# Two attention blocks on one core: group means through DRAM, the output bias on VectorE, a split first norm, earlier q blocks, and the first two scores together

## The chip, the core and the metric

The kernel runs on one core of one Trainium2 chip. All times are device microseconds (us) of that core. The engines are named as in the profile: PE is TensorE (matrix products; PEld is its weight loads), DVE is VectorE, ACT is ScalarE, POOL is GpSimd and SP is SyncE, which here only issues transfers (its queue is SPq). All data are fp32.

## What is computed

Two self-attention blocks follow each other on x of shape 8 x 512 x 32 x 32 (8 images, 512 channels, 1024 positions). Both have the same form, cut here to what matters:

```
def block(x, gamma, beta, wqkv, bqkv, wp, bp):        # x: (8, 512, 1024)
    xg   = x.reshape(8, 8, -1)                        # 8 groups of 64 channels
    mean = xg.mean(-1, keepdims=True)
    var  = xg.var(-1, keepdims=True)
    xn   = ((xg - mean) * rsqrt(var + 1e-5)).reshape(x.shape) * gamma + beta
    q, k, v = split(wqkv @ xn + bqkv)                 # 8 heads of 64 channels each
    attn = softmax(q.T @ k / 8)                       # over the keys
    o    = attn @ v
    return x + wp @ o + bp
```

The whole is `block(block(x, weights of layer 0), weights of layer 1)`.

## The kernel before

A **job** is one image in one layer. There are 16, ordered so that two images alternate: image 0 and 1 in layer 0, then both in layer 1, then images 2 and 3, and so on. The order of PE, ACT and DVE instructions is written out by hand: each of these engines executes them in the order in which the Python code emits them. A small planner helps. `later(delay, fn)` (L104) registers work for a planned clock time, and `advance(us)` (L107) moves that clock by the planned length of the PE work just emitted and emits what has come due. SP's and POOL's order isn't written out; a scheduler arranges it by dependencies and priority.

A job goes through four stages.

- **V phase** (`v_phase`, L371). The value projection is computed with seven products of half-size blocks instead of eight (Strassen's scheme in Winograd's form). `combine` (L277) makes the sums of blocks of the normalised input on DVE, `factor` (L147) the sums of weight blocks. Seven products by two groups of tokens give 14 steps, each planned at 1.72 us. While such sums of a weight are first made, the raw blocks are loaded, four DVE operations turn them into seven factors, and `store_factors` (L158) keeps the result in DRAM, from where `fetch` (L165) loads single factors into a ring of 8 buffers.
- **Projection phase** of the job before (`proj_phase`, L405): the output projection in the same scheme. It adds `out_bias`, a vector per layer that holds bp + wp @ bv.
- **Deep phase** (`deep_phases`, L442): the K and Q projections with the scheme applied twice, so 7 + 7 chains of seven products of 128x128 by 128x256. Two chains are interleaved. `prepare` (L184) makes a chain's inner factors (four small DVE operations) when they are used for the first time. In each chain (`chain`, L328) product 7 is added up in bank z, a put reads z, and product 4 is then added up in the same bank. The puts of products 7 and 3 are on DVE, the others on ACT.
- **Attention** (`Attention`, L582): 8 groups (4 head pairs by 2 halves of the queries) of 8 key chunks, 64 steps. `scores(i)` (L592) emits the scores product `sc`, the exponential `e` on ACT and, from the second chunk of a group on, the DVE addition into `acc` (L611, L613) for the softmax sums; `values(i)` (L615) emits the product `po` with v. `finish` (L632) turns a group's sums into reciprocals by way of two small transfers (`lr`, `rd`) and a broadcast (`rb`), and normalises q's columns in place. Work of the next job is inserted into the 64 steps as `chores`, keyed by step.

The group norm of job n+1 runs as chores in the attention of job n (`norm_steps`, L208). `stat` (L221) makes mean and variance of each channel on DVE, for one chunk of 128 channels at a time. `group_mean` (L226) multiplies by the block matrix `blk`, whose 64x64 blocks hold 1/64: a product `pm` for the mean and, with the deviations, a product `pvar` for the variance. Each uses a `sc` buffer of PSUM. POOL takes the power -1/2, DVE scales (L253) and ACT adds beta (L260).

`make_out_bias` (L742) computes wp @ bv with 16 products of 128x128 by 128x1, into `pb`, again a `sc` buffer. It runs as a chore of jobs 0 and 2.

The start (from L777) issues the loads of image 0, the V and K blocks and image 1; does the whole norm of job 0 alone; emits the first four of the 14 V steps, then the sums and factors, then the rest. The raw q blocks are loaded later (`second_blocks`, L816) into the buffer of raw k, whose tag `"k"` the first K result uses as well.

The end of a deep phase and the start of the attention are interleaved, with `both[-3:]` the products 7, 3 and 4 of the last chain:

```
896         att = Attention(att_n)
897         att.scores(0)
898         both[-3]()
899         att.scores(1)
900         both[-2]()
901         both[-1]()
```

Of the kernel before, what the change touches and what calls it, by code (L numbers as in the profile page):

```python
# [9 lines left out]
F32 = mybir.dt.float32  # L10
# [28 lines left out]
NW = 7  # L39
# [5 lines left out]
RING = 8  # L45

# [9 lines left out]
def make_constants(nc, const, env, vecs):  # L56
    env.vec_sb = const.tile([P, 2 * NVEC], F32, name="vec_sb")
    nc.sync.dma_start(env.vec_sb, vecs)
# [11 lines left out]
def fast_path(  # L70
    ctx: ExitStack, tc: tile.TileContext, env: Env, x: bass.AP, wqkv: list, wp: list,
    out: bass.AP,
# [92 lines left out]
    def fetch():  # L165
# [9 lines left out]
        src = factors[which, layer][:, FACTOR[o]]  # L175
        if which in (V, O):
            nc.sync.dma_start(wide(w), src)
        elif (which, layer, o) in deep:
            nc.sync.dma_start(w, deep[which, layer, o])
        else:  # L180
            nc.sync.dma_start(wide(w), src)
            raw.add(key)
# [19 lines left out]

    def load_x(b):
        xs[b] = xpool.tile([P, NC, S], F32, tag="x", name=f"x_{b}")
# [3 lines left out]
    def norm_steps(n, alone=False):  # L208


        b, layer = jobs[n]
        xt = xs[b]
        stats = small.tile([P, NC, 2, 6], F32, tag="stats", name=f"stats_{n}")
        mv = small.tile([P, NC, 2], F32, tag="mv", name=f"mv_{n}")
        dev = small.tile([P, NC], F32, tag="dev", name=f"dev_{n}")
        mean = small.tile([P, NC], F32, tag="mean", name=f"mean_{n}")
        var = small.tile([P, NC], F32, tag="var", name=f"var_{n}")
        mul = small.tile([P, NC], F32, tag="mul", name=f"mul_{n}")
        g0 = layer * NVEC + GAMMA

        def stat(cc):  # L221
            for sh in range(2):
                nc.vector.bn_stats(stats[:, cc, sh, :], xt[:, cc, sh * HALF : (sh + 1) * HALF])
            nc.vector.bn_aggr(mv[:, cc, :], stats[:, cc, :, :].rearrange("p s k -> p (s k)"))

        def group_mean(src, name):  # L226
            if alone:
                pm = bank(0, "z", name)
                nc.tensor.matmul(pm[:, :NC], env.blk, src, start=True, stop=True)
                return [(slice(0, P), pm[:, :NC])]  # L230
            pm = two_banks("sc", name)
            for h in range(2):
                r = slice(h * HD, (h + 1) * HD)
                nc.tensor.matmul(pm[r, h, :NC], env.blk[r, r], src[r], start=True, stop=True)
            return [(slice(h * HD, (h + 1) * HD), pm[h * HD : (h + 1) * HD, h, :NC]) for h in range(2)]

        def first():
# [909 lines left out]
```

## Time and profile before

| | |
|---|---|
| median of 3 runs | 3291.85 us (3286.91 to 3293.28) |
| the profiled execution | 3291.33 us, span 3289.6 us, mean granted PE clock 0.996 |
| PE busy | 3265.8 us, 99% of the span |
| DVE busy | 2588.4 us, 79% |
| ACT busy | 1729.2 us, 53% |
| POOL busy | 17.5 us, 1% |
| transfers | 262.80 MB, mean 80 GB/s |
| scores products `sc` (L602) | 1070.1 us busy, 8192 instructions |
| values products `po` (L627) | 1059.1 us busy, 8192 instructions |
| group-mean products `pm` and `pvar` in attention (L234) | 120 instructions of 0.17 to 0.20 us |
| output-bias products `pb` (L749) | 64 instructions of 0.25 us |
| first V product | at 16.54 us |
| first scores product | at 92.46 us |
| V phase to V phase, jobs 4 and 5 | 828.30 to 1030.78 us |

A product of fp32 operands shows as two PE instructions. The ends of matmuls in the profile are modelled, so distances between starts say more than durations. In lines of a timeline the columns are start in us, duration in us, engine, line, operation, output<-input, shape and count; what stands in brackets is the idle time of the engine before it and what released it. In lines of the table of waits the columns are the waiting engine, line and instruction, what it waited for, us in total, number of waits and the longest.

### The profile page before, as it was taken

To read this page: it belongs to the slowest core of one execution; us is meant where nothing else is said; L and a number is where in the kernel's file an instruction comes from. 1 tells how busy PE (TensorE), PEld (TensorE's weight loads), DVE (VectorE), ACT (ScalarE), POOL (GpSimd) and SP (SyncE) were. 2 spreads that over 40 slices of the span, in tenths; PEclk is the share of its full clock that TensorE was granted. 3 is DMA by queue.
4 is the path that set the end of the run, shared out by engine and by line. 5 is a ranking of instruction groups with operands and counts; after the bars stand their busy time and mean duration, and the time that the engine had idled before them with its cause. 6 is when DMAs were issued, how large, how long until landed. Compare 5 with 4: busy or idle time off the path is not lost.

```text
span 3289.6 us, 56485 instructions
## 1 busy us (share of the span) xinstructions
PE 3265.8 (99%) x22420; PEld 1748.7 (53%) x22420; DVE 2588.4 (79%) x3630; ACT 1729.2 (53%) x2557; POOL 17.5 (1%) x30
## 2 busy tenths in 40 slices
PE   8999999999999999999999999999999999999999
PEld 6456374563745637356373564735546365563643
DVE  7886978869688696877959779596895968869676
ACT  3555635556364563646636366463654636546363
POOL 0000000000000000000000000000000000000000
PEclk9999999999999999999999999999999999999999
DMA  7223142140411203023050221303214031130401
GB/s 279 83 80 114 66 144 74 52 145 22 162 31 59 86 19 117 28 76 118 22 171 22 76 66 34 113 17 110 85 35 161 19 93 49 41 105 22 127 28 45
DMA packets 142352, 262.80 MB, mean 80 GB/s; under 512 B 44544, under 2 KB 52736, under 8 KB 141056
## 3 DMA queue, kind: packets, MB, share of 16 engines
q1 hardware_dynamic: 142080, 259.12, 24.7%
q8 instruction: 178, 2.92, 0.4%
q14 instruction: 94, 0.77, 0.1%
HBM read 212.10 MB, written 44.83 MB: 78 GB/s over the span
## 4 chain that ended last, share of the span: by engine, by line
PE 97%; ACT 1%; DMA 1%; DVE 1%; issue 0%; SPq 0%; POOL 0%; DVEq 0%
PE sc L602 27%; PE po L627 26%; PE vd L486 8%; PE zd L486 7%; PE z L384 6%; PE z L419 6%; PE ud L486 3%; PE yd L486 3%; PE u L384 2%; PE y L384 2%; PE v L384 2%; PE u L419 2%; PE y L419 2%; PE v L419 2%; ACT e L607 1%; PE pp L571 1%
## 5 line engine op out<-in xcount | busy, mean ns | idle before, releaser
L607 ACT ACTIVATE e<-sc 128x1024 f32<-128x1024 f32 x1024 | 1047.4, 1023 | 626.5 <-PE sc L602 545.3
L602 PE MATMUL sc<-q,k 64*64 64x512 f32 x8192 | 1070.1, 593 | 6.6 <-ACT e L607 6.6
L627 PE MATMUL po<-e,v 64*64 64x512 f32 x8192 | 1059.1, 590 | 0.0
L613 DVE TENSOR_TENSOR acc<-acc,e 128x1024 f32<-128x1024 f32 x768 | 936.5, 1219 | 60.6 <-ACT e L607 11.0
L627 PEld LDWEIGHTS po<-e,v 64*64 64x64 f32 x8192 | 313.6, 133 | 568.1 <-issue 557.9
L602 PEld LDWEIGHTS sc<-q,k 64*64 64x64 f32 x8192 | 305.7, 133 | 548.5 <-issue 524.8
L486 PE MATMUL vd<-deep,w 128*128 128x256 f32 x960 | 269.7, 382 | 0.0
L486 PE MATMUL zd<-deep,w 128*128 128x256 f32 x832 | 233.0, 380 | 3.9 <-DVE p L502 3.9
L611 DVE TENSOR_TENSOR acc<-e,e 128x1024 f32<-128x1024 f32 x128 | 156.1, 1219 | 66.5 <-ACT e L607 65.5
L486 PEld LDWEIGHTS vd<-deep,w 128*128 128x128 f32 x960 | 181.7, 191 | 37.2 <-ACT p L498 13.0
L486 PEld LDWEIGHTS zd<-deep,w 128*128 128x128 f32 x832 | 158.1, 190 | 33.3 <-issue 6.9
L639 DVE TRANSPOSE_TENSOR_REDUCE r<-acc 128x32 f32<-128x1024 f32 x128 | 158.5, 1238 | 0.5
L335 ACT COPY yd<-vd 128x256 f32<-128x256 f32 x128 | 45.7, 357 | 187.0 <-PE vd L486 180.1
L426 DVE TENSOR_TENSOR s5o<-v,x 128x512 f32<-128x512 f32 x60 | 38.5, 684 | 101.3 <-PE v L419 101.3
L419 PE MATMUL z<-to,w 128*128 128x512 f32 x240 | 110.3, 592 | 0.0
L384 PE MATMUL z<-w,xn 128*128 128x256 f32 x480 | 110.1, 382 | 0.0
L384 PE MATMUL z<-w,t 128*128 128x256 f32 x480 | 108.5, 379 | 0.0
L419 PE MATMUL z<-q,w 128*128 128x512 f32 x240 | 107.9, 592 | 0.0
L669 DVE TENSOR_TENSOR q<-q,rb 128x512 f32<-128x512 f32 x128 | 86.6, 676 | 26.5 <-DMA rb<-rd 26.5
L384 PEld LDWEIGHTS z<-w,xn 128*128 128x128 f32 x480 | 90.0, 190 | 23.8 <-issue 12.2
L339 ACT COPY u<-z 128x512 f32<-128x512 f32 x62 | 35.3, 570 | 121.5 <-PE z L419 84.8
L384 PEld LDWEIGHTS z<-w,t 128*128 128x128 f32 x480 | 91.2, 190 | 12.4
(169 smaller groups left out, 3434.4 us busy)
## 6 DMA issues: line engine op xcount, KB each, us to landing
w<-deep SPq DMA_DIRECT2D x196, 448.0 KB, 3.3
w<-keep SPq DMA_DIRECT2D x238, 256.0 KB, 2.7
rb<-rd SPq DMA_DIRECT2D x256, 128.0 KB, 2.9
x<-x_dram SPq DMA_DIRECT2D x32, 512.0 KB, 6.2
out_dram<-x SPq DMA_DIRECT2D x64, 256.0 KB, 3.5
deep<-w SPq DMA_DIRECT2D x28, 448.0 KB, 2.9
keep<-raw SPq DMA_DIRECT2D x5, 1792.0 KB, 6.0
lr<-r SPq DMA_DIRECT2D x512, 4.0 KB, 1.7
```

Source lines behind the costliest of these rows:

```text
L335: nc.scalar.copy(y, z)
L384: nc.tensor.matmul(ps[:, ti * CH : (ti + 1) * CH], r[:, cc, t0 : t0 + P], w[:, cc, :], start=(start and ti == 0 and cc == 0), stop=(cc == ...
L419: nc.tensor.matmul(ps, w[:, cc, i * P : (i + 1) * P], r[:, cc, :], start=(start and cc == 0), stop=(cc == 1), skip_group_check=True,)
L426: nc.vector.tensor_add(s5[:, oh, :], ps, at(oh, 1))
L486: nc.tensor.matmul(ps, lhs[:, FACTOR[i], :], moving[i], start=start, stop=True, skip_group_check=True,)
L602: nc.tensor.matmul(sc[h * HD : (h + 1) * HD, j, :], k[r, hp, k0 : k0 + HD], q[r, hp, sh * HALF : (sh + 1) * HALF], start=True, stop=True,)
L607: nc.scalar.activation(e, sc, AF.Exp, scale=SCALE)
L611: nc.vector.tensor_add(acc[g], es[i - 1], e)
L613: nc.vector.tensor_add(acc[g], acc[g], e)
L627: nc.tensor.matmul(po[g][j * HD : (j + 1) * HD, h, :], v[r, kc, d0 : d0 + HD], e[r, j, :], start=(kc == 0), stop=(kc == NT - 1),)
L639: nc.vector.tensor_reduce(r, a.rearrange("p j (b e) -> p (j b) e", e=RP), AX.X, ALU.add, apply_transpose=True,)
L669: nc.vector.tensor_mul(q[:, hp, cols], q[:, hp, cols], rb)
```

## The change

1. **Group means.** For jobs 1 to 15, `norm_steps` no longer uses PE. A new chore at step 17 (`gather`) stores the channels' means and variances to DRAM and loads them back with a group's 64 channels in one row, on 8 partitions. At step 24 (`groups`) DVE makes mean and variance of each group, POOL takes the power, a transfer stores the 8 pairs to DRAM and two broadcasts bring them back to all partitions. Scaling starts at step 36 as before.
2. **Output bias.** `make_out_bias` loads the rows of wp and a broadcast bv into the buffers `acc` and `px`, and DVE multiplies and reduces, four times per layer. It is called after the attention of jobs 0 and 2 and comes due 19 us into the next V phase.
3. **Start.** Image 0 is loaded in half chunks, the first two chunks ahead of one V block and the vectors; then the other chunks and V blocks, K's and the raw q blocks, these into the buffer of image 1, whose own load moves to 30 us later on the planned clock. The norm of job 0 is made in two halves of 2 chunks each, with PE products as before (of 2 columns), and idle products of `blk` between them; the first V step stands before the second half's norm. The V steps run in the order 1, 5, 2, 6, 7, 3, 4. One sum of V's weights moves to POOL. The first K and Q fetches of factors 1, 2 and 4 read the input weights instead of the stored factors. K and Q go into one plan; the sums for chain products on combined inputs come 12 us into it instead of 7.5.
4. **First scores.** `att.scores(0)` and `att.scores(1)` are called one after the other, before the last three products of the deep phase.

```
@@ norm @@
+        def gather(self):
+            self.dm = dram.tile([NC, P, 2], F32, tag="dm", name=f"dm_{self.n}")
+            nc.sync.dma_start(self.dm.rearrange("c p k -> p c k"), self.mv)
+            self.gm = small.tile([GROUPS, HD, 2], F32, tag="gm", name=f"gm_{self.n}", bufs=1)
+            nc.sync.dma_start(self.gm, self.dm.rearrange("c (h p) k -> (c h) p k", h=2))
+
+        def groups(self):
...
+            nc.vector.bn_stats(gs, gm[:, :, 0])
+            nc.vector.bn_aggr(ga, gs)
+            nc.vector.tensor_reduce(gv, gm[:, :, 1], AX.X, ALU.add)
+            nc.vector.tensor_scalar(gv, gv, 1.0 / HD, EPS, ALU.mult, ALU.add)
+            nc.vector.tensor_add(gv, gv, ga[:, 1:2])
+            nc.gpsimd.tensor_tensor(ga[:, 1:2], gv, env.neg_half[:GROUPS, 0:1], ALU.pow)
+            dg = dram.tile([GROUPS, 2], F32, tag="dg", name=f"dg_{n}")
+            nc.sync.dma_start(dg, ga)
             for h in range(2):
...
+                src = dg.rearrange("(c h) k -> h c k", h=2)[h : h + 1]
+                nc.sync.dma_start(
+                    self.mr[h * HD : (h + 1) * HD], src.to_broadcast([HD, NC, 2])
+                )
@@ output bias @@
+        for i in range(2):
+            nc.sync.dma_start(
+                rows[i], wrows[layer][i * CH : (i + 1) * CH].rearrange("(oc p) c -> p oc c", p=P)
+            )
+        nc.sync.dma_start(bvb, bv[layer : layer + 1, :].to_broadcast([P, C]))
+
+        def part(oc):
+            r = rows[oc // 2][:, oc % 2, :]
+            nc.vector.tensor_mul(r, r, bvb)
+            nc.vector.tensor_reduce(out_bias[:, layer, oc : oc + 1], r, AX.X, ALU.add)
...
-                nc.tensor.matmul(
-                    pb[:, 0, oc : oc + 1], w[:, at, cc % 2, o0 : o0 + P],
-                    env.vec(layer, BV, cc), start=(cc == 0), stop=(cc == NC - 1),
-                )
...
+            if n in (0, 2):
+                make_out_bias(jobs[n][1], 19.0)
@@ start @@
+    load_chunk(0)
+    load_chunk(1)
+    env.load_vecs()
+    load_block(v0, V, 0, 0)
+    load_chunk(2)
+    load_chunk(3)
+    for i, j in ((1, 0), (1, 1), (0, 1)):
+        load_block(v0, V, i, j)
     load_blocks(k0, 0, K)
-    load_x(1)
+    load_blocks(q0, 0, Q)
...
+    norm.stat(0)
+    norm.stat(1)
+    mean, var = norm.means_by_products(0, lambda: idle_products(0, "y", "again_a"))
+    mean()
+    var()
+    for i in range(3):
+        idle_products(i % 2, "y", f"again_b{i}")
+    norm.stat(2)
+    norm.factors(slice(0, 2))
+    normed((0, 1), left)
+    normed((0, 1), right_)
+    nc.gpsimd.tensor_add(v0[:, S1], v0[:, S3], v0[:, A22])
+    norm.stat(3)
+    first[0]()
+    mean, var = norm.means_by_products(1, lambda: None)
...
+    deep_sums(0, 0.2, 12.0)
+    later(5.0, first_plan)
     for part in range(4):
...
+        later(16.0 + 0.9 * part, lambda part=part: factor(q0, part))
+    later(20.0, lambda: store_factors(q0, 0, Q))
+    later(21.0, lambda: store_factors(v0, 0, V))
+    later(30.0, lambda: load_x(1))
@@ first scores @@
         att.scores(0)
-        both[-3]()
         att.scores(1)
-        both[-2]()
-        both[-1]()
+        for thunk in both[-3:]:
+            thunk()
```

## The prediction

> **What bounds the kernel now.** I read the busy times and the chain of waits first, then the table of waits of TensorE (PE), then the timeline around each place that the change touches.
>
> ```profile
> PE 3265.8 (99%) x22420; PEld 1748.7 (53%) x22420; DVE 2588.4 (79%) x3630; ACT 1729.2 (53%) x2557; POOL 17.5 (1%) x30
> PE 97%; ACT 1%; DMA 1%; DVE 1%; issue 0%; SPq 0%; POOL 0%; DVEq 0%
> PE sc L602 <- ACT e L607: 6.6, 30, 0.2
> PE zd L486 <- DVE p L502: 3.9, 3, 3.4
> PE z L384 <- ACT xn L259: 3.6, 1, 3.6
> PE vd L486 <- DMA w<-keep: 1.5, 1, 1.5
> ```
>
> PE is the bound. VectorE (DVE) at 79% and ScalarE (ACT) at 53% lie beside it. Three of the four waits belong to the first 75 us; the fourth is 30 short stops at the group-mean products. So an edit is worth the PE time that it takes away, or the PE stop that it makes.
>
> A whole job (an image and a layer) takes 202.48 us from one V phase to the next (828.30 to 1030.78 in the chain in order of time). Around a group-mean product the timeline of PE reads (start, duration):
>
> ```profile
> 344.47 1.04 PE L627 MATMUL po<-e,v 64*64 64x512 f32 x8
> 345.33 0.24 PE L234 MATMUL pm<-mv,blk 64*64 64x4 f32 x4
> 345.80 1.09 PE L602 MATMUL sc<-q,k 64*64 64x512 f32 x8 [0.22 <-ACT e L607]
> 346.70 1.04 PE L627 MATMUL po<-e,v 64*64 64x512 f32 x8
> 347.74 1.09 PE L602 MATMUL sc<-q,k 64*64 64x512 f32 x8
> ```
>
> Groups normally start 0.858 us apart. The output-bias product of job 0, in the same view:
>
> ```profile
> 117.69 1.04 PE L627 MATMUL po<-e,v 64*64 64x512 f32 x8
> 118.66 4.68 PE L749 MATMUL pb<-vec_sb,raw 128*128 128x1 f32 x32
> 123.27 1.98 PE L602 MATMUL sc<-q,k 64*64 64x512 f32 x8
> 126.74 1.69 PE L602 MATMUL sc<-q,k 64*64 64x512 f32 x8
> ```
>
> And two windows at the start (stretch; PE, PEld, DVE, ACT and POOL busy; PEclk; DMA):
>
> ```profile
> 59.79:63.20 3.41, 1.20 (x6) 1.07 (x7) 3.38 (x9) 0.82 (x3) 0.00 (x0) 1.00 0.87 284
> 63.20:66.61 3.41, 3.41 (x10) 2.70 (x9) 2.94 (x8) 1.07 (x4) 0.00 (x0) 0.50 0.94 358
> ```
>
> After a stretch of 3.41 us in which PE worked 1.20 us (35%), the next 3.41 us ran at half clock.
>
> **What the Trainium skill says.** "TensorE: Matmul & The Clock Gate", section Part 1 (What's actually happening): a free-running window of 3413 ns sets the clock, which halves after an idle window and returns after a busy one. The trace agrees on the length and the factor, but 35% busy was already idle enough. "DMA: Bandwidth & Descriptors", Anatomy of one DMA: a fixed cost of about 2.0 us, mostly the write's receipt; here the 4 KB stores rd<-rt land in 1.3 us and lr<-r in 1.7. "Perfetto Trace Analysis", Tensor Engine Instruction: DVE and ACT are strict FIFO. This decides the last edit below.
>
> **Group means.** Each pm puts the later groups off: sc at 347.74 should, with 0.858 spacing, have been at 347.05, and the po after it (348.65) at 347.90, so 0.75 us. Each pvar the same way: po 361.18 against 360.67, 0.51. The 15 norms of jobs 1 to 15 lose both: 15 x 1.26 = **18.9 us off**. Added: per norm 5 small SP transfers. SP is in order, so the read of dm waits about 2 us for its store with the next lr loads behind it; the broadcasts wait for dg the same way. Consumers are 7 steps (12 us) and 12 steps (20 us) later. The lr queued behind has about 1 us to spare (issued 336.84 to 339.3, 1.7 us to land, read at 342.10), so DVE may wait 0.5 to 1 us in each norm; exponentials have five buffers and DVE only accumulates from them, so PE sees nothing. DVE does 5 small operations instead of 7, POOL the same power (1.0 us). I take 0; the bounds are 0 and 1 us a norm.
>
> **Output bias.** After pb the next groups start at 123.27, 125.03, 126.74, 128.25 (po, full clock again); without it the last would be at 117.69 + 4 x 0.858 = 121.12. That is 7.13 us; the second (job 2) goes from 530.79 to 541.34 by the same count, 7.12. **14.3 us off**, a third of it at half clock. Added on DVE: 8 products and reductions, about 0.68 us each from the 128x512 adds, so 11 us over two jobs, from the end of the V phase into the projection, where DVE is busy 11.39 of 24 us (440 to 464). Three SP loads of 1.25 MB, issued a phase earlier. Cost 0, at most 2 us.
>
> **Start.** In order of time, durations from the rows of before. (1) Two of four channel chunks are normalised first. Before: statistics end 11.24, first V product 16.54, then 16 products at half clock until 22.99 instead of 3.45. After: two chunks' statistics cost 3.0 us from about 4, end 7.0; the mean and variance chain 2.9 us to the end of the power; statistics of chunk 2 share that time and delay the factors to 10.5; four half scales and shifts, PE about 12.3. The idle products keep PE busy, so I take full clock. (2) PE then waits for the second half's shifts nowhere for long: by my queue of DVE instructions the right-hand combinations are ready at 16.3, 19.6 and 22.1, when PE asks at 16.4, 19.9 and 23.3. The V phase's last-but-one step ends at 23.3 + 7 x 1.725 = 35.4, against 42.15, and the first K weights come straight from the inputs, so the 1.5 us wait for w<-keep goes: 8.3 us. (3) The deep phase from there to the first scores took 92.46 - 43.67 = 48.8 us against 43.2 of work (1.725 + 96 x 0.431): 5.6 lost, from the k write waiting for raw_q's store (same buffer) and the half-clock window. Raw q moves to an x buffer, so that goes too. New: the preparations of w for products 6 and 5 stand on DVE before the first puts and need K's store (5 to 8 us from 28.4) plus a 2.7 us load: DVE is held to about 39, PE then stops about 1.5 and 2.0 us, with half a chance of a slow window: 4.7. SP's other moves (V store ahead of K's, q blocks ahead, x 1 after q's store, needed only at about 95) are hidden behind the deep phase. Gain 8.3 + 5.6 - 4.7 = **9.2 us off**, bounds 4 and 14.
>
> **Both first scores together.** The end of a deep phase and start of an attention before, on all queues:
>
> ```profile
> 505.55 1.09 PE L602 MATMUL sc<-q,k 64*64 64x512 f32 x8
> 506.57 0.70 PE L486 MATMUL vd<-deep,w 128*128 128x256 f32 x2
> 506.71 1.02 ACT L607 ACTIVATE e<-sc 128x1024 f32<-128x1024 f32 x1 [0.58 <-PE sc L602]
> 507.31 0.48 DVE L502 SCALAR_TENSOR_TENSOR p<-vd,vec_sb,s 128x256 f32<-128x256 f32 x1 [0.66 <-PE vd L486]
> 508.76 0.59 PE L486 MATMUL vd<-deep,w 128*128 128x256 f32 x2
> 509.28 1.09 PE L602 MATMUL sc<-q,k 64*64 64x512 f32 x8
> 509.42 1.23 DVE L611 TENSOR_TENSOR acc<-e,e 128x1024 f32<-128x1024 f32 x1 [0.49 <-ACT e L607]
> ```
>
> The second vd (product 4) accumulates in the bank that DVE reads in the put at 507.31, so it waits for it. scores(1) issues the first sum acc; called before the three products, it puts acc on DVE **ahead of that put** (the changed kernel's DVE order shows it). New times: second scores 505.55 + 0.86 = 506.41; first exponential 506.71 to 507.73, second to 508.71; acc from 508.75; the put 1.14 later (so far apart two such adds start, 348.19 and 349.33), 509.9 to 510.38; vd at 510.42, third scores 0.52 later, 510.95. Before they began at 509.28: **1.67 us more in each of 16 attentions, 26.7 us**. Two saved switches between tile shapes (0.1 to 0.2 each) are already in this. ACT and the later sums catch up inside the wait.
>
> The wait leaves PE idle about 2.0 us in one piece. Fully inside a clock window, with the switch gaps, it leaves 30 to 40% busy, about the 35% that halved the clock; 65% (56.38 to 59.79) did not. A slow window costs 3.41 / 2 = 1.71. The job then repeats every 202.48 - 1.26 + 1.67 + 1.71 = 204.60 us = 59.94 windows, so a job once caught has nearly the same phase next time; uncaught, 202.89 us shifts it by 0.44 window. I take 12 of 16 caught: **20.5 us**, bounds 0 and 27.
>
> **Rivals**, all from the median 3291.85; the profiled execution (3291.33, span 3289.6) is at it, the others 3286.91 and 3293.28.
> - Forecast: 3291.85 - 18.9 - 14.3 - 9.2 + 26.7 + 20.5 = 3296.7, say 3296; own range 3286 to 3304. Chance 0.50.
> - The clock stays full, since the idle piece straddles windows or the threshold is lower: 3276. For it: 1.5 us at 43.67 did not lower it. Against: 35% did. Chance 0.27.
> - The edit doesn't do what I read: put and product stay unhindered, all savings remain, 3249. Only if acc's wait were met early, which two exponentials of 1.02 forbid. Chance 0.05.
> - Slower: every attention is caught (27.3) and the start gives back all but 4, by K's store reaching DVE late: 3291.85 - 33.2 - 4 + 26.7 + 27.3 = 3308.6. It decides once 14 windows are slow with the start under 5. For it: the lock of phase. Against: DMA has free time there. Chance 0.18.
>
> **Numbers.** What can be told from no change is 0.2%, 6.6 us. The forecast lies 4 us above before with some 6 us of its own doubt: 0.02 faster, 0.29 same, 0.19 slower. The second gives 0.26 faster and 0.01 same, the third 0.05 faster, the fourth 0.17 slower and 0.01 same. Sum 0.33, 0.31, 0.36. The range 3268 to 3307 leaves out the third and half of the fourth, 0.14.
>
> **What would show it.** No pm or pvar but in the first 20 us, no pb; V phase to V phase 202.9 or 204.6; at each attention's start PE stopped about 2 us on the put behind acc; PEclk 0.5 for 3.41 us after it; first scores at about 83. I am wrong if that stop is under 1 us, if the clock stays full in most jobs, or if DVE waits for gm or mr with PE behind it.

## The result and the profile after

The changed kernel takes 3315.36 us (median of 4 runs, 3313.62 to 3317.93) against 3292.57 of the kernel before (4 runs on the same chip, 3286.91 to 3293.37): ratio 1.0074, 95% interval 1.0056 to 1.0091. It is 22.8 us **slower**. The forecast was 3296 with a range to 3307, so the time lies outside it. The profiled execution has a span of 3312.6 us, 23.0 more than the one before.

First the page of the changed kernel, the busy times and the chain of work that ended last, by engine:

```profile
PE 3257.2 (98%) x22240; PEld 1726.5 (52%) x22240; DVE 2588.3 (78%) x3625; ACT 1729.6 (52%) x2561; POOL 25.2 (1%) x32
...
PE 74%; DVE 17%; issue 4%; DMA 3%; SPq 1%; ACT 1%; DVEq 0%; POOL 0%; ACTq 0%
```

PE has 8.6 us less to do than before (3265.8) and yet the span is longer. The chain says where it went: 97% of it was PE before, now 17% is DVE and 3% DMA. Another engine sets the end in long stretches. Three rows of the table of waits (waiting instruction, releaser, total us, times, longest us) name the places:

```profile
DVE lt L706 <- DMA lr<-r: 75.7, 47, 4.1
...
PE vd L535 <- DVE p L551: 30.3, 17, 1.8
...
PE v L433 <- DVE q L698: 11.8, 10, 2.6
```

The second row is the forecast's stop at the head of each attention, that is, between its first and its third scores. The first was in the forecast only as 0.5 to 1 us in each of 15 norms: DVE waits for the row-sum loads lr (7.0 us in 15 waits before). The third was not in it at all: PE stops in the V phase for an addition that DVE makes late.

The head of job 11's attention, in order of time:

```profile
2345.84 1.94 ACT L656 ACTIVATE e<-sc 128x1024 f32<-128x1024 f32 x2 [0.57 <-PE sc L651]
...
2347.81 1.23 DVE L660 TENSOR_TENSOR acc<-e,e 128x1024 f32<-128x1024 f32 x1 [2.03 <-ACT e L656]
2348.95 0.48 DVE L551 SCALAR_TENSOR_TENSOR p<-vd,vec_sb,s 128x256 f32<-128x256 f32 x1
...
2349.48 0.70 PE L535 MATMUL vd<-deep,w 128*128 128x256 f32 x2 [1.79 <-DVE p L551]
```

DVE itself waits 2.03 us for two exponentials, then does the sum, then the put, and PE waits 1.79 us for the put. From the first to the third scores it is 5.43 us, against 3.73 before. Two windows there (stretch; PE, PEld, DVE, ACT and POOL busy; PEclk; DMA share, GB/s):

```profile
2347.09:2350.50 3.41, 1.62 (x9) 0.69 (x11) 2.69 (x4) 0.97 (x2) 0.00 (x0) 1.00 0.00 0
2350.50:2353.91 3.41, 3.41 (x20) 1.07 (x16) 2.69 (x4) 1.22 (x2) 0.00 (x0) 0.50 0.34 82
```

The whole stop lies in one stretch of 3.41 us, in which PE works 47% of the time; the next stretch runs at half clock. That happens at the heads of 8 of 16 attentions, and in jobs 10 to 14 at five heads in a row, the first three of them 204.85 us apart.

Last the missed part, from job 6: SP's issues, DVE's wait, and 60 us later PE.

```profile
1370.51 1.40 POOL L252 TENSOR_TENSOR ga<-gv,neg_half 8x1 f32<-8x1 f32 x1 [201.75 <-DMA rb<-rd]
1371.44 1.23 DVE L688 TRANSPOSE_TENSOR_REDUCE r<-acc 128x32 f32<-128x1024 f32 x1
1371.94 0.28 SPq L254 DMA_DIRECT2D dg<-ga  x1
1373.11 1.27 SPq L257 DMA_DIRECT2D mr<-dg  x2
1374.47 2.46 SPq L694 DMA_DIRECT2D lr<-r  x4
1381.72 0.36 DVE L706 TENSOR_REDUCE lt<-lr 32x32 f32<-32x128 f32 x1 [4.09 <-DMA lr<-r]
...
1441.66 0.65 DVE L698 TENSOR_TENSOR q<-po,px 128x512 f32<-128x512 f32 x1
...
1442.36 1.99 PE L433 MATMUL v<-w,t 128*128 128x256 f32 x8 [1.14 <-DVE q L698]
```

r is ready at 1372.67, but SP first has the store of dg and the two broadcasts mr to issue. lr goes out at 1374.47 to 1376.93 and lands almost 5 us after its last issue. DVE stands still for 4.09 us and waits for nothing more until the V phase, whose second product then waits 1.14 us for DVE's last addition out of the banks that it needs.

The whole difference, from the starts of the stages in both traces (after less before):

| place | us |
|---|---|
| start, up to the first scores (83.16 against 92.46) | -9.3 |
| 16 heads, first to third scores, 1.70 each | +27.2 |
| 8 half-clock windows at heads, 1.7 each | +13.6 |
| attention without group-mean products, 15 x 1.03 | -15.5 |
| attention without output-bias products, 2 x 7.13 | -14.3 |
| V start to first scores (89.41 us in nearly all jobs before, 89.4 to 93.9 after) | +17.4 |
| job 0's attention 2.0, job 7's 0.5, the last part 1.1 | +3.6 |

The sum is 22.7 of 23.0 us. Of the 17.4, 1.7 is a half-clock window in job 0's V phase (206.96 to 210.37), right behind a stop of 2.58 us. The 1.03 us could be read in the kernel before already: its last attention, the only one without a norm, takes 108.31 us from the third scores to its end, most of the others 109.34.

### The profile page after: what moved, and what is told of

It is laid out like the page before. It is cut to its first block, busy times and chain, and to the rows that moved or that the text cites. A ratio compares the mean times of both kernels' runs of the same rounds, so it can differ in the third digit from the quotient of the medians.

```text
span 3312.6 us, 56298 instructions
## 1 busy us (share of the span) xinstructions
PE 3257.2 (98%) x22240; PEld 1726.5 (52%) x22240; DVE 2588.3 (78%) x3625; ACT 1729.6 (52%) x2561; POOL 25.2 (1%) x32
## 4 chain that ended last, share of the span: by engine, by line
PE 74%; DVE 17%; issue 4%; DMA 3%; SPq 1%; ACT 1%; DVEq 0%; POOL 0%; ACTq 0%
PE sc L651 17%; PE po L676 16%; DVE acc L662 9%; PE vd L535 8%; PE zd L535 7%; PE z L468 6%; PE z L433 5%; PE yd L535 3%; PE ud L535 3%; DVE acc L660 2%; DMA lr<-r 2%; PE v L468 2%; PE y L468 2%; PE u L468 2%; PE y L433 1%
## 5 line engine op out<-in xcount | busy, mean ns | idle before, releaser
L433 PE MATMUL z<-w,t 128*128 128x256 f32 x480 | 108.6, 379 | 0.6 <-DVE v L448 0.6
L706 DVE TENSOR_REDUCE lt<-lr 32x32 f32<-32x128 f32 x128 | 46.3, 362 | 75.7 <-DMA lr<-r 75.7
```

The lines of the kernel that those rows point to most:

```text
L433: nc.tensor.matmul(ps[:, ti * CH : (ti + 1) * CH], r[:, cc, t0 : t0 + P], w[:, cc, :], start=(start and ti == 0 and cc == 0), stop=(cc == ...
L706: nc.vector.tensor_reduce(lt, lr.rearrange("p a b -> p b a"), AX.X, ALU.add)
```

## The experiments

Fifteen kernels. "Stop at V start" is the sum of what the 15 stretches from V start to first scores take over 89.41 us, half-clock windows in them included; "slow heads" counts the attentions whose head or first steps hold a half-clock window; "waits for lr" is DVE's row in the table of waits. Each kernel's ratio is to runs of the kernel before on the same chip. The medians of those runs lie between 3288.6 and 3292.6, so the difference of two kernels that were timed beside different runs is sure to a few us only. Numbers 1 to 4 shared theirs, as did 5 to 8, 9 to 12, and 13 to 15.

| | kernel | us, median | ratio, 95% interval | stop at V start | slow heads | waits for lr |
|---|---|---|---|---|---|---|
| | before | 3288.6 to 3292.6 | 1 | 0.8 | 0 | 7.0 |
| | changed | 3315.36 | 1.0074 (1.0056, 1.0091) | 18.2 | 8 | 75.7 |
| 1 | transfers on GpSimd's queue | 3307.76 | 1.0058 (1.0044, 1.0072) | 8.2 | 10 | 44.1 |
| 2 | transfers at other steps | 3328.93 | 1.0118 (1.0102, 1.0133) | 8.9 | 15 | 33.5 |
| 3 | first scores apart | 3271.93 | 0.9944 (0.9931, 0.9958) | 17.1 | 0 | 70.9 |
| 4 | put ahead of the sum | 3270.38 | 0.9946 (0.9932, 0.9959) | 14.2 | 0 | 69.6 |
| 5 | start alone | 3282.03 | 0.9974 (0.9964, 0.9985) | 0.9 | 0 | 9.6 |
| 6 | start and round trip | 3286.11 | 0.9986 (0.9980, 0.9993) | 19.5 | 0 | 74.6 |
| 7 | number 2, stop filled | 3310.44 | 1.0059 (1.0045, 1.0073) | 9.8 | 0 | 33.4 |
| 8 | number 4, GpSimd's sums | 3280.74 | 0.9973 (0.9962, 0.9984) | 7.6 | 0 | 40.0 |
| 9 | apart, two ways of means | 3256.97 | 0.9903 (0.9888, 0.9918) | 0.9 | 0 | 13.2 |
| 10 | number 8 without GpSimd's sums | 3267.90 | 0.9935 (0.9922, 0.9949) | 12.5 | 0 | 26.9 |
| 11 | GpSimd's queue, few packets | 3303.70 | 1.0042 (1.0028, 1.0055) | 1.5 | 15 | 14.4 |
| 12 | before, scores together | 3326.05 | 1.0113 (1.0097, 1.0128) | 2.1 | 6 | 9.8 |
| 13 | few packets on SP | 3305.50 | 1.0050 (1.0037, 1.0064) | 6.9 | 13 | 39.0 |
| 14 | apart, GpSimd's queue, few packets | 3254.91 | 0.9897 (0.9882, 0.9912) | 1.7 | 0 | 16.1 |
| 15 | apart, all means by PE | 3269.07 | 0.9941 (0.9928, 0.9955) | 0.9 | 0 | 12.6 |

### 1. The group means' transfers on GpSimd's queue

```
-            nc.sync.dma_start(self.dm.rearrange("c p k -> p c k"), self.mv)
+            nc.gpsimd.dma_start(self.dm.rearrange("c p k -> p c k"), self.mv)
```

and the same for gm, dg and the two mr.

> The changed kernel, with the group means' transfers (dm, gm, dg, mr) issued by GpSimd instead of SP; all else stays. My theory (the queue): on SP they hold up the row-sum loads lr behind them, VectorE waits for lr (75.7 us in all), is late by the end of the attention, and TensorE stops in the second product of the V phase on q<-po. Then the waits of VectorE for lr fall from 75.7 to under 20 us, the stop of TensorE on q<-po is gone, and the time from V start to first scores goes back to 89.4 us, 17 us less in all: 3298, up to 10 more if the more regular jobs make more heads of attention fall into half-clock windows (then 8 to 14 such windows). Rival (no slack): VectorE is simply full in the attention once TensorE no longer does the group means; then the waits for lr fall but the stop on q<-po stays near 11.8 us: 3312 to 3318. Rival (landing): the small packets make lr land late from whichever queue; waits for lr stay above 50 us, time 3312 to 3318.

Measured 3307.76. The waits for lr fell to 44.1, not under 20, and the stop at the V start to 8.2 us, 6.6 of it in jobs 0 to 2. The theories of the queue and of the landing were each half right. No slack alone is out, since the stop follows the waits (none in jobs 3 and 4, where the waits fell from 5.9 and 5.6 us to 3.0 and 0.5; 0.9 in job 5, where they are 5.0; waits are counted here from one V start to the next), and the queue alone is out too, since more than half of the waits stayed. The rest shows in the DMA rows of this kernel (KB each, median us from issue to landing) and in its wait:

```profile
lr<-r SPq DMA_DIRECT2D x512, 4.0 KB, 1.7
mr<-dg POOLq DMA_DIRECT2D x30, 2.0 KB, 5.5
```

```profile
1160.07 3.65 SPq L694 DMA_DIRECT2D lr<-r  x4
...
1162.08 1.29 POOL L257 DMA_DIRECT2D mr<-dg  x2 [1.90 <-DMA dg<-ga]
```

lr leaves at once here, but its four issues take 3.65 us instead of 2.46, mr goes out among them, and DVE waits 3.94 us for lr, until 1168.95; the median of 1.7 us over all 512 lr doesn't show such a one. A broadcast of 2 KB takes 5.5 us to land. The Trainium skill says in "DMA: Bandwidth & Descriptors", Rules for kernel authors, that transfers issued from different engines run on the same 16 DMA engines and interleave. The trace agrees as far as it goes: with another queue, 44.1 of the 75.7 us of waits stay.

### 2. The same transfers on SP, at other steps

```
-                chores = dict(zip((4, 8, 12, 16, 17), reads))
-                chores.update(zip((24, 36, 40, 44, 48, 52), steps))
+                chores = dict(zip((4, 8, 12, 20, 22), reads))
+                chores.update(zip((30, 36, 40, 44, 48, 52), steps))
```

> The changed kernel, with the transfers left on SP but at other steps of the attention: last statistics at step 20 instead of 16, gather at 22 instead of 17, groups at 30 instead of 24, so that in SP's order dm comes behind lr of group 1 and dg and mr behind rd and rb of group 2. Theory of the queue: the same as with GpSimd's queue, 3298 (to 3308), waits for lr under 20 us, no stop on q<-po. No slack: 3312 to 3318, stop stays. Landing: also 3298, since the small packets now fall in other stretches than lr; so where this one gains and GpSimd's queue doesn't, it is the landing.

Measured 3328.93, 11 us above the highest range that any theory had given (3312 to 3318). From job 3 on the theory of the queue holds: of 33.5 us of waits 21 belong to jobs 0 to 2, and from job 4 on each V phase reaches its first scores in 89.41 us. Two other things took the gain and more. In jobs 0 to 2 the shifted transfers, together with a store of prepared weights, put lr far back on SP:

```profile
149.79 1.30 SPq L257 DMA_DIRECT2D mr<-dg  x2
151.18 0.55 SPq L161 DMA_DIRECT2D keep<-raw  x1
162.11 0.35 SPq L177 DMA_DIRECT2D w<-keep  x1
162.51 2.46 SPq L694 DMA_DIRECT2D lr<-r  x4
...
166.19 0.36 DVE L706 TENSOR_REDUCE lt<-lr 32x32 f32<-32x128 f32 x1 [8.81 <-DMA lr<-r]
...
168.56 1.02 ACT L656 ACTIVATE e<-sc 128x1024 f32<-128x1024 f32 x1 [8.27 <-DVE acc L662]
...
169.64 1.98 PE L651 MATMUL sc<-q,k 64*64 64x512 f32 x8 [6.85 <-ACT e L656]
```

The load w waits on SP for the store of keep, 10.3 us, and lr stands behind it; DVE then waits 8.81 us, the next exponential 8.27 us for DVE's sum (its buffer is not free before), and PE stops 6.85 us for it. And now that no stop at the V start moves them, all jobs from 4 on repeat every 204.79 us, and 15 of 16 heads are slow, against 8.

### 3. First scores apart

```
         att.scores(0)
+        both[-3]()
         att.scores(1)
-        for thunk in both[-3:]:
-            thunk()
+        both[-2]()
+        both[-1]()
```

> The changed kernel with the first scores apart again (scores 0, product 7 of the last chain, scores 1, products 3 and 4), all else as changed. My theory: heads (first to third scores) back from 5.43 to 3.73 us, 27.2 us less in 16 attentions; the 8 half-clock windows at the heads go too, 13.6 us; the stop on q<-po at the V start stays, since the transfers are as they were, and comes back in the jobs whose head had hidden it: 0 to 8 us more. Sum 3315.4 - 40.8 = 3275, range 3270 to 3284. Rival: the stop at the V start is a consequence of the late heads, and goes with them: 3257.

Measured 3271.93, 43.4 below the changed kernel and within the range. Heads are 3.73 us again, no head is slow, and the stop at the V start stays at 17.1 us. So it is no consequence of the late heads, and the edit on the first scores is the greatest loss in the change.

### 4. The put ahead of the sum

```
-        att.scores(1)
-        for thunk in both[-3:]:
-            thunk()
+        att.scores(1, add=False)
+        both[-3]()
+        att.add(1)
+        both[-2]()
+        both[-1]()
```

`add` holds the lines that issue the sum acc.

> The changed kernel, both first scores still together on TensorE, but the first sum of exponentials (acc) is put on VectorE behind the put of product 7 instead of ahead of it. My theory: the stop comes from VectorE's order alone; so TensorE's stop on that put falls from 1.8 to under 0.5 us, heads take 3.4 to 3.7 us, half-clock windows at the heads go; 3272 (3265 to 3282), at or a little under the kernel with the scores apart, for the saved switches of tile shape. Rival: the two scores standing together are the cost (third scores wait for the second exponential, or the put itself waits for TensorE's products that now start later): heads stay above 4.5 us and the time above 3295.

Measured 3270.38. PE's order is that of the changed kernel; only two DVE instructions have changed places. Job 0's head:

```profile
84.70 0.48 DVE L551 SCALAR_TENSOR_TENSOR p<-vd,vec_sb,s 128x256 f32<-128x256 f32 x1 [1.61 <-PE vd L535]
...
85.24 0.70 PE L535 MATMUL vd<-deep,w 128*128 128x256 f32 x2 [0.21 <-DVE p L551]
...
86.23 1.22 DVE L667 TENSOR_TENSOR acc<-e,e 128x1024 f32<-128x1024 f32 x1
```

The stop of 1.79 us is 0.21, the head 3.85 us, a little over the 3.4 to 3.7 expected. So the loss came from DVE's order alone, as forecast; with it in order, scores together are no faster than apart (3.85 against 3.73).

### 5. The start alone

The first norm, early q blocks and block weights as changed; the other three edits as before.

```
-        reads = ... + [norm.gather]          # means by products, as before
-        steps = [norm.groups]
+        steps = [first, second]
-            if n in (0, 2):
-                make_out_bias(jobs[n][1], 19.0)
+            if which == O:
+                chores[at] = ...             # bias by products, as before
```

and the first scores apart.

> Of the change only the start is left (first norm in two halves, q blocks loaded early, block weights straight from the inputs): group means and output bias by TensorE and the first scores apart, as before. My prediction's term: 9.2 us less than before (bounds 4 and 14), first scores at 83 instead of 92.46; 3280. Rival: the early loads crowd the later ones and half of the gain is given back by job 1 (more than 4 us later at its V phase): 3285.

Measured 3282.03, first scores at 81.65, nothing given back later. 8.7 us below the runs of before beside it (3290.7).

### 6. The start and the round trip

Number 5 with `gather` and `groups` put back.

> The same plus the group means by the round trip through DRAM; against the kernel with the start alone it shows that edit alone, against the one with the first scores apart the output bias alone. By the traces so far an attention without the group-mean products is 1.03 us shorter on TensorE (15.4 in all), and the stops at the V start with VectorE's waits for lr give about 10 back (job 1 about 4.5, jobs 3 to 15 about 5.5; in jobs 0 and 2 the output-bias product leaves VectorE the time): 5 us less than the start alone, 3275 (3270 to 3281). If the transfers cost nothing, as I predicted: 19 less, 3261.

Measured 3286.11: 4.1 us **more** than the start alone, where 5 less were expected. The edit alone makes the kernel slower. The attentions are 1.03 us shorter, but the stop at the V start is 19.5 us. I had thought that the output-bias product would leave DVE time in jobs 0 and 2; they lose 4.4 and 2.0 us all the same. That product comes before lr is late, and time that DVE gets early in an attention it can't save, since it then waits for the next exponential (2.73 us at 115.95 in job 0). Against number 3, which has the bias on DVE besides, it is 14.2 us slower: the output bias gained about what was forecast (14.3).

### 7. The stop filled with products

On number 2, four products that nobody reads, into the unused half of a bank, between products 3 and 4:

```
+        for i in range(4):
+            nc.tensor.matmul(spare[0], env.blk,
+                env.blk.unsqueeze(1).to_broadcast([P, 2, P]),
+                start=True, stop=True, skip_group_check=True)
         both[-1]()
```

> The kernel with the shifted steps (3328.9 us), with four products of 128x256 that nobody reads put on TensorE between products 3 and 4 of the last chain, that is into its stop at the head of each attention; they go to the unused half of a bank. Heads keep their 5.4 to 5.8 us. Theory (clock): the stop is what lowers the clock in the window after it, and the lock keeps all 13 jobs from the third on in it; then the half-clock windows at the heads go, V start to V start falls from 204.79 to about 203.0 from job 3 on, and the time by 13 to 15 times 1.7: 3304 (3300 to 3310). Rival: the longer attentions come from something else (VectorE or ScalarE late); then the period stays at 204.8 and the time at 3325 to 3332.

Measured 3310.44, 18.5 below number 2 and at the upper end of the range for the clock; the rival wanted 3325 or more. One head:

```profile
1538.47 0.59 PE L536 MATMUL ud<-t,w 128*128 128x256 f32 x2
1538.90 1.89 PE L1007 MATMUL zd<-blk 128*128 128x256 f32 x8
1540.86 0.70 PE L536 MATMUL vd<-deep,w 128*128 128x256 f32 x2
```

The head still takes 5.43 us, but no head is slow and a job takes 203.15 instead of 204.79 us. PE does more and the kernel is faster: the half-clock windows come from PE's idle time, not from DVE's or ACT's delay as such, and cost 1.64 us a job.

### 8. GpSimd's sums of weight blocks

Number 4, the transfers shifted from job 3 on, and in jobs 0 to 2:

```
-                chores[at] = lambda ...: factor(box[0][:, i], part)
+                chores[at] = lambda ...: factor(box[0][:, i], part, nc.gpsimd)
```

> The changed kernel with the put ahead of the sum of exponentials (3270.4 us), the transfers of the group means shifted to the later steps in the attentions of jobs 3 and after, and in jobs 0 to 2 the sums of weight blocks, which prepare the factors of the next weights, done by GpSimd instead of VectorE (1.27 us each instead of 0.68, 8, 8 and 4 of them). Theory: VectorE is full in the attention, so every microsecond of wait or work that is put on it there comes out at the V start; the stops of TensorE there (14 us and one half-clock window in the kernel with the put first) go to under 3 us: 3256 (3252 to 3261), the fastest so far. Rival: in jobs 0 to 2 it isn't VectorE's work but the stores of the factors and loads that are in the way: gain of jobs 3 and after alone, about 4 us, 3266.

Measured 3280.74, 10 us slower than number 4. From job 5 to job 11 the jobs take 201.57 us without a stop, as expected, but the attentions of jobs 0 and 1 take 117.8 and 118.1 us from the third scores to the V start, against 110.8 and 108.6. POOL, DVE and SP in job 0:

```profile
98.69 2.26 POOL L152 TENSOR_TENSOR raw<-raw 128x512 f32<-128x512 f32 x1
101.03 2.15 POOL L154 TENSOR_TENSOR raw<-raw 128x512 f32<-128x512 f32 x1
```

```profile
95.51 6.53 DVE L670 TENSOR_TENSOR acc<-acc,e 128x1024 f32<-128x1024 f32 x3
...
107.16 3.85 DVE L670 TENSOR_TENSOR acc<-acc,e 128x1024 f32<-128x1024 f32 x3
```

```profile
106.67 0.34 SPq L162 DMA_DIRECT2D keep<-raw  x1
107.11 0.37 SPq L178 DMA_DIRECT2D w<-keep  x1
107.53 4.33 SPq L702 DMA_DIRECT2D lr<-r  x4
```

Neither theory named this. The eight sums run as soon as their blocks are there, 91.79 to 106.64, and while they run three of DVE's additions take 6.53 us, which take 3.85 once GpSimd is done: in these 6.5 us GpSimd makes about three sums, which would have taken DVE 0.68 us each, and DVE loses 2.7. And the store of keep comes 38 us earlier than in number 4 (144.58), just ahead of lr, whose four issues take 4.33 us; DVE waits 3.07 us there, and didn't in number 4. How much of the 10 us belongs to each of the two is not shown.

### 9. Apart, with means by products in the crowded attentions

Number 3; the norms of jobs 1 to 3, which run in the attentions of jobs 0 to 2, take their means by products on PE as before, the later ones by the round trip at the steps of number 2.

```
+        steps = [first, second] if n <= 3 else [norm.groups]
```

> The changed kernel with the first scores apart (3271.9 us); the norms of jobs 1 to 3, whose attentions also carry the sums of weight blocks, get their group means by products on TensorE as before; the later norms keep the round trip, at the shifted steps. Theory: what is left to win over the kernel with the first scores apart are TensorE's stops at the V start (4.5, 5.1 and 2.0 us in jobs 0 to 2, 5.5 in the later jobs together) and the two half-clock windows behind them (3.4): 20.5 less, 3.1 more for the products of three norms, 1 to 3 left in jobs 0 to 2, where VectorE stays nearly full: 3256 (3253 to 3262), about 35 under the kernel before. Rival: in jobs 0 to 2 VectorE is late by its own work, without any wait for lr: 6 to 9 us of the stops stay there, 3263 to 3266.

Measured 3256.97, as expected. The stop at the V start is 0.9 us and the later jobs take 201.45 us.

### 10. Number 8 without GpSimd's sums

> The changed kernel with the put ahead of the sum (3270.4 us) and the transfers shifted in the attentions of job 3 and later; jobs 0 to 2 as changed, the sums of weight blocks on VectorE. It is the kernel of 3280.7 us without GpSimd's sums. Theory: those sums (2.2 us each beside VectorE's work, and earlier than planned) cost the 8 and 10 us in the attentions of jobs 0 and 1; without them they are 108.3 to 110.8 us again, and of the stops at the V start those of the later jobs (3.7) are gone: 3267 (3264 to 3270). Rival: the shift in the later jobs brought the loss with it: 3275 or more.

Measured 3267.90, as expected: GpSimd's sums cost 12.8 us (3280.74 less 3267.90), and the shift in the later jobs gains 2.5 over number 4.

### 11. GpSimd's queue and few packets

Number 1, with the groups in another order in dg, so that a partition's four pairs of mr come in one piece of 32 bytes instead of four of 8:

```
-            nc.gpsimd.dma_start(self.gm, self.dm.rearrange("c (h p) k -> (c h) p k", h=2))
+            nc.gpsimd.dma_start(self.gm[:NC], self.dm[:, :HD])
+            nc.gpsimd.dma_start(self.gm[NC:], self.dm[:, HD:])
...
-                src = dg.rearrange("(c h) k -> h c k", h=2)[h : h + 1]
+                src = dg.rearrange("(h c) k -> h (c k)", h=2)[h : h + 1]
...
-                    self.mr[h * HD : (h + 1) * HD], src.to_broadcast([HD, NC, 2])
+                    self.mr[h * HD : (h + 1) * HD].rearrange("p c k -> p (c k)"),
+                    src.to_broadcast([HD, 2 * NC]),
```

> The kernel with the group means' transfers on GpSimd's queue (3307.8 us; waits for lr 44.1 us), with the groups in another order in dg, so that each partition gets its 4 pairs of mr in one piece of 32 bytes instead of four of 8: 128 packets for the two broadcasts instead of 512; gm is read in two transfers. Theory (the half that the queue doesn't explain is landing): lr lands late beside mr's many small packets; so mr's median from issue to landing falls from 5.5 to under 3.5 us and VectorE's waits for lr from 44 to 20 to 30; the time hardly changes (3300 to 3310), since half-clock windows at the heads follow the period. Rival (landing has nothing to do with the packets): the waits stay at 40 to 48 us.

Measured 3303.70; waits for lr 14.4 us, fewer than expected, and no stop at the V start but 0.7 and 0.8 in jobs 0 and 1 (job 1 had 0.8 before the change). GpSimd's queue in number 1 and here (packets, MB, share of the time of 16 DMA engines), and the broadcast here:

```profile
q0 software_dynamic: 2400, 0.19, 1.5%
```

```profile
q0 software_dynamic: 2880, 0.19, 0.2%
...
mr<-dg POOLq DMA_DIRECT2D x30, 2.0 KB, 2.2
```

Nearly the same bytes keep the DMA engines busy for about an eighth of the time, and the broadcast lands in 2.2 us instead of 5.5. It is not the count of packets that fell: on this queue the profile shows more of them than in number 1, as gm is read in two transfers and one packet of mr holds several pieces. What fell is the time of a packet, and "few packets" stands for few pieces here. The time gained is only 4 us, since now 15 heads are slow.

### 12. Both first scores together in the kernel before

The diff of number 3 the other way round, on the kernel before.

> The kernel before with this one edit: both first scores ahead of the last three products. The prediction's two terms alone: heads 3.73 to about 5.43 us, 27.2 us in 16 attentions, and 1.6 us for each head whose stop lowers the clock. A job then repeats every 204.18 us (59.8 windows of 3.413) where the clock stays full and 205.8 (60.3) where it falls, so that the stop doesn't keep its place in the window as it does at 204.8 (60.0): I expect 5 to 9 of 16 heads with a half-clock window, 8 to 14 us, and no stop at the V start: 3290.7 + 27.2 + 11 = 3329 (3325 to 3333). If every such stop lowers the clock, whatever its place: 16, 26 us, 3344. If the two terms were wrong and the loss of the change lies elsewhere: under 3305.

Measured 3326.05, 37.3 above the kernel before and within the range. Heads 5.43 us, 6 of them slow, none twice in a row: a job takes 204.19 us when its head is not slow and 205.83 when it is, and neither is a whole number of windows of 3.413 us. Where a job takes 204.79 to 204.85 (60.0 windows) they come in rows, as in numbers 2, 11 and 13. So the stop must have its place in the window, and the period of the job decides whether it keeps it. The traces of the six kernels with this stop (changed, 1, 2, 11, 12, 13) show the place. The half-clock windows of a trace start whole multiples of 3.413 us apart, which gives the window's edges for all 96 heads. In 69 of them the stop of 1.79 us lay inside one window, and 67 were slow; in 27 it crossed an edge, and none was slow.

### 13. Few packets on SP

The edit of number 11 on the changed kernel, with all transfers left on SP.

> The changed kernel, transfers on SP and at their steps as they are; only the packets are fewer (groups in another order in dg, each partition's 4 pairs of mr in one piece of 32 bytes: 128 packets for the two broadcasts instead of 512; gm in two reads). It tells the two halves of the missed term apart. If lr's place behind the transfers in SP's order is one half and landing beside mr's packets the other: VectorE's waits for lr fall from 75.7 to between 30 and 50 us, stops at the V start stay in jobs 0 to 2. If the packets are all of it: waits under 20 us, as with GpSimd's queue and few packets (14.4), and no stop on q<-po. If the order is all of it: waits over 60. The time follows the half-clock windows at the heads and stays between 3303 and 3318 in each case.

Measured 3305.50; waits for lr 39.0, and of 6.9 us of stops 6.0 in jobs 0 and 1. Neither cause is the whole: place in SP's order and landing beside small packets each hold a little under half of the 75.7 us (39.0 without the packets, 44.1 without the place, 14.4 without both).

### 14. Apart, GpSimd's queue, few packets

Numbers 3 and 11 together.

> The first scores apart, the group means' transfers on GpSimd's queue with few packets, the rest as changed. Theory: no stop at the V start but 0.8 us in jobs 0 and 1, no half-clock window after the start, an attention of 108.31 us in the jobs 2 to 15 and none of the products of group means: 3 us under the best so far (3257.0), 3254 (3251 to 3257). Rival: with the scores apart VectorE has less time in the attention and the stops of jobs 0 to 2 come back: 3260 or more.

Measured 3254.91, the fastest: 1.0% below the kernel before (ratio 0.9897). Its page:

```profile
PE 3240.5 (100%) x22240; PEld 1729.7 (53%) x22240; DVE 2592.4 (80%) x3625; ACT 1729.7 (53%) x2561; POOL 79.1 (2%) x122
...
PE 97%; DVE 2%; DMA 0%; issue 0%; ACT 0%; SPq 0%; POOL 0%; DVEq 0%
```

The chain is PE again. Three of the change's four parts stay in it.

### 15. Apart, all means by products

Number 14 without any transfer.

> The same without any transfer: first scores apart, all group means by products on TensorE as before, start and output bias as changed. Its difference to the kernel with few packets on GpSimd's queue is the worth of the round trip where it disturbs nothing: by the attentions 15 times 1.03 = 15.4 us, so 3269 (3266 to 3272); by my prediction's term 18.9, 3273. Its difference to the kernel of the start alone (3282.0) is the output bias: 14.3 by my prediction, less about 1 us of stop in job 0 or 1: 3268 to 3269.

Measured 3269.07. The round trip is worth 14.2 us where it disturbs nothing (15 x 1.03 expected), the output bias 13.0 against number 5.

## Why the prediction was wrong

The sum was 4.8 us and the result 22.8. By its own steps:

| step of the prediction | predicted | measured |
|---|---|---|
| start | -9.2 | -9.3 in the trace, -8.7 in time (number 5) |
| output bias | -14.3 | -14.2 (6 against 3), -13.0 (15 against 5) |
| group-mean products off PE | -18.9 | -15.5 in the trace, -14.2 in time (15 against 14) |
| transfers of the group means | 0, at most 1 a norm (15 in all) | +17.4, from 0 to 4.5 a job |
| first scores together | +26.7 | +27.2 |
| slow-clock windows | +20.5 (12 of 16) | +13.6 (8 of 16) |

**The step that failed** is the cost of the round trip, "DVE may wait 0.5 to 1 us in each norm; exponentials have five buffers and DVE only accumulates from them, so PE sees nothing ... I take 0". It failed twice. The wait is 3.6 to 6.7 us in most jobs: of the queue I had counted the place of lr behind the transfers (about half), and not that lr lands beside them, for which the kernel before had no row. And PE does see it. An attention gives DVE 7.5 us free (101.89 us busy of 109.35 in job 3 before). When half of that or more is gone in mid-attention, the delay is carried to the end, where the V phase takes over the banks from which DVE has to add first. I asked who waits for DVE during the attention and not who takes over the banks after it. The cure of both halves brings the stop from 18.2 to 1.5 us (number 11), and with it the edit is worth 14.2 us (15 against 14); as it was changed, it costs 4 (6 against 5). Nor do five buffers hide every wait: in number 2 one of 8.81 us held up the next exponential and PE in mid-attention.

**The size of the group-mean products** was read from the groups next to them, 0.75 and 0.51 us. The attention as a whole is 1.03 shorter in each of 15 jobs, so the term was 3.4 to 4.7 us too large. Two stops of 0.22 us at the products make up part of the local count, and where the difference is made good is not shown; the last attention of the kernel before had the right number.

**The slow-clock windows** were the right mechanism with too high a count. A stop of 1.8 us inside one window leaves PE 47% busy, where 30 to 40% were forecast, and halves the next one (number 7 takes the idle time away and the windows go). That the stop must lie fully inside one window, as the prediction said, is so in all 67 slow heads of number 12's count. The lock that the prediction worked out, 204.60 us or 59.94 windows, is there at 204.85. What I had not allowed for is that the stop at the V start, up to 4.5 us, shifts the jobs against the windows, so only jobs 10 to 14 stayed locked. That makes the two terms exchange: every cure of the V start alone (1, 2, 11, 13) brought 10 to 15 slow heads. They took back part of its gain (in the traces the stop fell by 10.0, 16.7 and 11.3 us in 1, 11 and 13, and the span by 7.6, 10.3 and 5.8); number 2, which also stops PE in jobs 0 to 2, lost more than all of it.

**Right** were the start, the output bias and the first scores, these down to the instruction: the put behind the sum on DVE (number 4). That the start came out at 9.3 for 9.2 has luck in it. Up to the first product of the deep phase it gained 6.7 us (43.67 to 36.93) where 8.3 were forecast, and from there to the first scores 2.6 where 0.9 were, since PE stopped there for 0.70 and 1.64 us, less than forecast, and no half-clock window followed. The sign of the sum, 4.8 us slower, lay within the prediction's own doubt of some 6 us. The rival on the other side, 3308.6, had the direction by chance: it wanted 16 slow heads and a start that gains 4.

## What to carry to other kernels

A transfer that is put on a queue can cost not only its place ahead of others but also their landing: count its pieces, not its bytes, and make each partition's piece contiguous. When an engine is said to have slack, ask where the slack lies and who takes over its buffers at the end of the stage; a wait in the middle is not absorbed by a free microsecond at the start. Before trusting a cure by its time, look at the granted clock: a gain can be taken back by idle pieces that fall into step with the clock's windows.

## What the runs showed of the hardware

- A window in which PE was busy 1.62 of 3.41 us (47%) was followed by one at half clock. The Trainium skill, "TensorE: Matmul & The Clock Gate", Part 1, gives an idle window as the condition; the measurement decides, and the window need not be idle.
- The busy share in the profile doesn't settle it alone. In the changed kernel the stretch 503.88 to 507.29, with 1.61 us busy, was followed by a full clock; in the kernel before the stretch 117.77 to 121.18, busy 3.41 of 3.41 us, mostly with the output bias's products of one column each, was followed by two windows at half clock.
- Of 69 stops of 1.79 us that lay inside one window 67 were followed by a half-clock window, of 27 that crossed an edge none.
- Jobs of 204.79 to 204.85 us, 60.0 windows, kept the half clock at up to 14 heads in a row (number 11); at 204.19 and 205.83 it never came twice in a row (number 12).
- On GpSimd's queue a 2 KB broadcast in pieces of 8 bytes to 64 partitions landed in 5.5 us (number 1), in pieces of 32 bytes in 2.2 (number 11).
- Beside DVE, GpSimd's eight additions of 128x512 took 1.27 to 2.27 us (1.27 in the start), and three of DVE's of 128x1024 beside them 6.53 us instead of 3.85. The Trainium skill, "GPSIMD Engine Reference", Specifications, has the two engines share their way to the on-chip memory, with contention where a DVE instruction has two inputs there; the trace agrees, as DVE's sums read two tiles each, and shows that DVE pays as well.
